# Two outlook-attention layers in fp32: bands of an image in one read, loads of x on another queue, and the first pair's transposed copies kept in idle buffers

## The chip, the core and the metric

The kernel runs on one core of one Trainium2 chip. The metric is device time in microseconds (us) from start to end of one execution, and the median of several executions is compared. All numbers are fp32.

The engines of a core are named as the profile names them: PE (TensorE, the matrix array), DVE (VectorE), ACT (ScalarE), POOL (GpSimd) and SP (SyncE, which only issues transfers here). ACT issues transfers too. An engine executes its own instructions in order; the engines wait for each other and for transfers through semaphores. SBUF is the on-chip memory of 128 partitions, PSUM the memory that PE writes.

## The reference

The input x has 8 images of 56 x 56 positions and 384 channels. Two layers follow each other, each of the form x + conv(groupnorm(x)) with 32 groups.

```
# layer 0, 12 heads of 32 channels, kernel 3 x 3, padding 1
v    = x @ Wv.T                               # padded by 1 in both directions
a    = (x @ Wa.T) as (position, head, 9, 9)
attn = softmax(a * 32 ** -0.5, last axis)
out  = for each position, head:  attn (9 x 9) @ the 3 x 3 patch of v
y    = fold(out)                              # adds each of the 9 rows at its offset
x    = x + y @ Wo.T
# layer 1, 6 heads of 64 channels, 9 weights a head
a    = softmax((x @ W_attn + b_attn) as (position, head, 9))
y    = sum over the 9 of the patch of v, weighted by a
x    = x + y @ W_proj + b_proj
```

The group norm needs the mean and the variance of 12 channels over a whole image before the first position of that image can be projected.

## The kernel before, in words

**Tiling.** Two images make a pair; a column of a pair has R = 112 rows, which lie on the partitions. There are four pairs of W = 56 columns. A block is XB = 4 columns, so a pair has NBLK = 14 blocks. The 384 channels are NCH = 3 chunks of 128.

**Statistics of pair 0.** Before the loop, `stats_load` (L389) reads a block of x as xr, in rows, on SP's queue. `stats_chunk` (L395) transposes it chunk by chunk on PE, with four transposes for each chunk. ACT copies the result to xt (L409), DVE takes the statistics (L411), and SP stores xt to xT in DRAM (L413). The pools hold two buffers for xr and two for xt. `norm_params` (L233) then averages over the groups with products by `gmat`, all nine pairs of chunks, and makes scale and bias. The group size is 12 and a group that crosses from one chunk to another reaches only the next chunk, so the blocks of gmat with chunk numbers two apart hold zeros. For the other pairs the same chunks are worked through inside the loop, one for each step, while the pair before is computed (`upkeep`, L651).

**Layer 0's loop.** A step is one column. `attend` (L476) makes three groups of 9 x 36 logits from xn and wa_t into PSUM banks; DVE, ACT and POOL make the softmax; the product with wv_t gives v, which ACT sends to the table vtab. `presum` and `fold` (L513, L543) sum rows and send the folded weights wt to a table ztab in DRAM. `load` (L457) brings back block g of xT as xin on SP's queue, and `normed` (L465) scales it into xn, which holds eight columns; `load(g)` stands six steps and `normed(g)` two steps ahead of the block's first column. Every seven columns `fetch_v` (L566) reads patches of v as vp, and `fetch` (L574) reads the bands of weights z, puts the contraction (pc) and the output product (po) in a list of jobs due four steps later, and reads the residual xres from xT. z has one buffer for each image of the pair, vp two.

**Bands.** `bands` (L304) reads one image's z in three transfers, given by `GROUPS0` (L88) as ranges of partitions and of target rows: partitions 0 to 48 with rows 0 to 5, 48 to 80 with rows 0 to 7, and 80 to 128 with rows 3 to 7. What is not read stays at the zeros that POOL writes into both z at the start (L455).

**Order.** PE's instructions are kept in program order, and so are the clears of the tables (`fill`, L176). All else is ordered by a scheduler, so a transfer can stand far from its place in the text. In the built program every transfer signals one of eight completion semaphores, which SP's and ACT's transfers take in turn; an issue also waits until the transfer that used its semaphore before has landed.

**Layer 1** works in the same way with its own tables and is not touched.

Of the kernel before, what the change touches and what calls it, by code (L numbers as in the profile page):

```python
# [8 lines left out]
F32 = mybir.dt.float32  # L9
# [6 lines left out]
def two_outlook_layers(  # L16
# [68 lines left out]
    PY1, NPY1, SX1, SY1 = 8, 7, PX + 2, 10  # L85
    ROW1 = HEADS1 * PX

    GROUPS0 = (((0, 48), (0, 5)), ((48, 80), (0, 7)), ((80, P), (3, 7)))  # L88
    GROUPS1 = (((0, 45), (0, 5)), ((45, 90), (3, 8)))


# [28 lines left out]

    def transpose(*args, **kwargs):
        tc.keep_in_program_order(nc.tensor.transpose(*args, **kwargs))  # L122


    ident = const.tile([P, P], F32, name="ident")
# [50 lines left out]
    def fill(table, first, dims, width):  # L176

        src = zeros[: dims[0][1], :width]
        if len(dims) > 1:
            src = src.unsqueeze(1).to_broadcast([dims[0][1], dims[1][1], width])  # L180
        tc.keep_in_program_order(
            nc.sync.dma_start(bass.AP(table.tensor, table.offset + first, [*dims, [1, width]]), src)
        )

    def clear_v(table, sx, pad):

        line = sx * C
        part = line // 12
        fill(table, 0, [[(R + GAP) * line, NPX + 1], [part, 12 * GAP]], part)
        fill(table, GAP * line, [[line, R], [C, pad]], C)  # L190
        fill(
            table, ((NPX - 1) * (R + GAP) + GAP) * line + (sx - pad) * C,
            [[line, R], [C, pad]], C,
        )

    def clear_weights(table, line, part, sx, slot, row, first, e, ep):
        fill(table, 0, [[part, MARGIN * line // part]], part)
        fill(table, (MARGIN + R) * line, [[part, (MARGIN + 1) * line // part]], part)
        top = MARGIN * line
        fill(table, top, [[line, R]], first * row)  # L200
        fill(table, top + (first + e) * row, [[line, R], [slot, sx]], (ep - e) * row)

    def clears():

        yield 0, lambda: clear_v(vtab0, SX0, 2)

        yield 0, lambda: fill(
            ztab0[0], MARGIN * LINE0 + FIRST0 * ROW0, [[LINE0, R], [SLOT0, 2]], E0 * ROW0
        )
        for n, t in enumerate(ztab0):  # L210
            yield (1, 2 * PX, 3 * PX)[n], lambda t=t: clear_weights(
                t, LINE0, 366, SX0, SLOT0, ROW0, FIRST0, E0, EP0
            )
# [11 lines left out]
    eps_t = const.tile([P, 1], F32, name="eps_t")  # L225
    nc.gpsimd.memset(eps_t, EPS)

    def weight(pool, src, n, name):
        t = pool.tile([P, NCH, n], F32, name=name)
        nc.sync.dma_start(t, src.rearrange("(i p) n -> p i n", p=P))  # L230
        return t

    def norm_params(st, name, params, key):  # L233

        mv = stat.tile([P, NCH, IMG, 2], F32, tag="mv", name=f"mv_{name}")

        def over_groups(src, what):
            pg = ps.tile([P, NCH, IMG], F32, tag="t", name=f"p{what}_{name}")
            for j in range(NCH):
                for i in range(NCH):  # L240
                    matmul(
                        pg[:, j, :], gmat[:, i, j * P : (j + 1) * P], src[:, i, :],
                        start=(i == 0), stop=(i == NCH - 1),
                    )
            g = stat.tile([P, NCH, IMG], F32, tag=what, name=f"{what}_{name}")
            nc.vector.tensor_copy(g, pg)
            return g

        for i in range(NCH):
            for b in range(IMG):  # L250
                nc.vector.bn_aggr(mv[:, i, b, :], st[:, i, b, :, :])
# [6 lines left out]
        nc.vector.tensor_add(part, part, mv[:, :, :, 1])  # L258
# [59 lines left out]
    class Jobs:  # L318


        def __init__(self):
            self.queue = []
# [30 lines left out]
    def patch_tiles(name, b):  # L353
        return patch.tile([P, NPY0, C], F32, tag="vp", name=f"vp_{name}_{b}")
# [25 lines left out]
    def layer0(late, pools):  # L380
# [5 lines left out]

        stats, st1s, params, xins, attns, pres, xrs, xts = {}, {}, {}, {}, {}, {}, {}, {}

        def stats_load(pair, blk):  # L389
            nm = f"{pair}_{blk}"  # L390
            xr = io.tile([P, XB, C], F32, tag="xr", name=f"xr_{nm}")[:R]
            nc.sync.dma_start(xr, xf[pair * R : (pair + 1) * R, blk * XB : (blk + 1) * XB, :])
            xrs[pair, blk] = xr

        def stats_chunk(pair, blk, i, alone):  # L395

            nm = f"{pair}_{blk}"
            if blk == 0 and i == 0:
                stats[pair] = stat.tile([P, NCH, IMG, NBLK, 6], F32, tag="st0", name=f"st0_{pair}")
            if i == 0:  # L400
                xts[pair, blk] = io.tile([P, NCH, XB, R], F32, tag="xt", name=f"xt_{nm}")
            xr, xt = xrs[pair, blk], xts[pair, blk]
            if alone:
                pt = bank(P, 0, XB * R).rearrange("p (m r) -> p m r", m=XB)
            else:
                pt = ps.tile([P, XB, R], F32, tag="t", name=f"pt_{nm}_{i}")
# [5 lines left out]
            if i == NCH - 1:  # L412
                nc.sync.dma_start(  # L413
                    xTs[pair][:, :, blk * XB * R : (blk + 1) * XB * R], xt.rearrange("p i m r -> p i (m r)")
                )
                del xrs[pair, blk], xts[pair, blk]

        stats_load(0, 0)
        for blk in range(NBLK):
            if blk + 1 < NBLK:  # L420
                stats_load(0, blk + 1)
            for i in range(NCH):
                stats_chunk(0, blk, i, True)
        for _ in norm_params(stats.pop(0), "0_0", params, 0):
            pass

# [22 lines left out]
                )  # L449
        for t in banks:  # L450
            nc.vector.memset(t[:, BANK - NP0 + NL :], 0.0)
        wv_t = weight(fixed, wv0, C, "wv0_t")
        wo_t = weight(late_w, wo0, C, "wo0_t")
        for z in zs:
            nc.gpsimd.memset(z, 0.0)  # L455

        def load(g):  # L457
            pair, blk = divmod(g, NBLK)
            xins[g] = io.tile([P, NCH, XB, R], F32, tag="xin", name=f"xin_{g}")
            nc.sync.dma_start(  # L460
                xins[g].rearrange("p i m r -> p i (m r)"),
                xTs[pair][:, :, blk * XB * R : (blk + 1) * XB * R],
            )
# [187 lines left out]
        def upkeep(step):  # L651

            pair, c = divmod(step, W)
            while clearing and clearing[0][0] <= step:
                clearing.pop(0)[1]()
            if pair + 1 < NPAIR:
                blk, i = divmod(c - 3, NCH)
                if 0 <= c and i == 0 and blk < NBLK - 1:
                    stats_load(pair + 1, blk + 1)
                if 3 <= c and blk < NBLK:  # L660
                    stats_chunk(pair + 1, blk, i, False)
                elif NBLK * NCH + 3 <= c < NBLK * NCH + 6:
                    if c == NBLK * NCH + 3:
                        making["0"] = norm_params(stats.pop(pair + 1), f"0_{pair + 1}", params, pair + 1)
                    next(making["0"])
            g, j = divmod(step + XB + 2, XB)
            if j == 0 and g < NPAIR * NBLK:
                load(g)
            g, j = divmod(step + 2, XB)
            if j == 0 and g < NPAIR * NBLK:  # L670
                normed(g)

        load(0)
        load(1)
        normed(0)
        LAG = 3
        for step in range(NPAIR * W + LAG):
# [329 lines left out]
```

## Time and profile before

| | |
|---|---|
| median of 12 runs | 3619.28 us (3612.08 to 3640.48) |
| the profiled execution | 3618.46 us, its span 3616.5 us |
| PE busy | 3465.0 us, 96% |
| DVE, ACT, POOL busy | 53%, 32%, 27% |
| DMA moved | 799.46 MB, 221 GB/s on average |
| SP's queue (q1), ACT's queue (q10) | 602.16 MB, 192.66 MB |
| first product of layer 0's loop | at 88.45 us |

PE's busy time is that of instructions in flight, so a busy PE is not a PE at its peak. An engine's idle time before an instruction is put down to what released it, in the form "<-DMA xr<-in_x": released by the transfer that wrote xr from in_x. The form "LABEL x12" means twelve instructions in one line. L119 and L122 are the helper lines by which all products and all transposes are recorded, so they are told apart by their tiles. "bank<-wa_t,xn" is a product of layer 0's logits, "pt<-ident,xr" a transpose inside the loop and "bank<-ident,xr" one of the start.

### The profile page before, as it was taken

The page shows a single profiled execution, that of the slowest core. Times are in us where ns is not written, and L with a number is a line of the kernel's source. Part 1 is how long each engine was busy: PE and PEld are TensorE (multiplying, and loading weights), DVE is VectorE, ACT ScalarE, POOL GpSimd, SP SyncE. Part 2 cuts the span into 40 slices and gives each one's busy share as a digit, 9 for nine tenths or more (in the row PEclk, how much of TensorE's full clock was granted, in tenths as well). Part 3 has the DMA queues.
Part 4 walks back from the last instruction along what each step waited for, and adds up shares of the span by engine and source line. Part 5 has one row for each costly group of instructions (what it writes and reads, how often), then busy time and mean ns, then how long its engine had stood idle before and what let it go on. Part 6 is the DMA issues. An engine that isn't in the chain of part 4 may idle for free. (4 is left out here: it accounts for less than half of the span.)

```text
span 3616.5 us, 72464 instructions
## 1 busy us (share of the span) xinstructions
PE 3465.0 (96%) x29078; PEld 2379.5 (66%) x29078; DVE 1915.8 (53%) x4648; ACT 1167.8 (32%) x2727; POOL 982.0 (27%) x1409
## 2 busy tenths in 40 slices
PE   5999899999999999999999999979999999999998
PEld 4667667767777677777777776645565565556555
DVE  3766566666776676666766666622222222222222
ACT  3333332333233233323322332223333333334332
POOL 2544333433444433343444444410000000000000
PEclk5999999999999999999999999989999999999998
DMA  8699999989999889999878887887787888788876
GB/s 283 202 261 260 251 255 233 221 207 241 252 228 235 213 217 236 248 256 216 205 192 203 211 216 194 193 241 186 207 222 204 223 216 217 198 223 209 220 190 154
DMA packets 694302, 799.46 MB, mean 221 GB/s; under 512 B 304270, under 2 KB 647374, under 8 KB 689870
## 3 DMA queue, kind: packets, MB, share of 16 engines
q1 hardware_dynamic: 359438, 602.16, 63.6%
q10 hardware_dynamic: 334528, 192.66, 22.0%
q8 instruction: 229, 3.75, 0.5%
q14 instruction: 107, 0.88, 0.1%
HBM read 473.04 MB, written 321.66 MB: 220 GB/s over the span
## 5 line engine op out<-in xcount | busy, mean ns | idle before, releaser
L119 PE MATMUL bank<-wa_t,xn 128*112 128x288 f32 x4032 | 1086.0, 409 | 3.3 <-ACT xn L471 2.2
L119 PEld LDWEIGHTS bank<-wa_t,xn 128*112 128x112 f32 x4032 | 693.9, 177 | 254.3 <-issue 32.8
L510 POOL TENSOR_TENSOR at<-at,den 112x972 f32<-112x972 f32 x224 | 503.7, 2249 | 1229.3 <-DVE den L509 1195.9
L119 PE MATMUL po<-yT,wo_t 128*128 128x448 f32 (+1 forms) x2304 | 821.8, 496 | 5.4 <-DVE x1t L621 4.8
L119 PEld LDWEIGHTS po<-yT,wo_t 128*128 128x128 f32 x2304 | 434.8, 191 | 294.8 <-issue 190.6
L119 PE MATMUL pc<-z,vp 121*32 121x49 f32 (+1 forms) x17664 | 492.5, 255 | 56.1 <-issue 25.6
L119 PEld LDWEIGHTS pc<-z,vp 121*32 121x32 f32 (+1 forms) x17664 | 445.1, 131 | 135.6 <-issue 107.4
L119 PE MATMUL bank<-wc_t,xn 128*128 128x438 f32 x1176 | 489.3, 553 | 3.0 <-ACT xn L740 3.0
L486 DVE TENSOR_REDUCE mx<-bank 112x36 f32<-112x324 f32 x672 | 326.5, 486 | 283.4 <-PE bank L119 277.3
L119 PE MATMUL bank<-wv_t,xn 128*128 128x384 f32 x1176 | 417.6, 492 | 2.6 <-DVE at L487 1.9
L487 DVE TENSOR_TENSOR at<-bank,mx 112x324 f32<-112x324 f32 x672 | 329.2, 490 | 20.7
L491 ACT ACTIVATE at<-at 112x972 f32<-112x972 f32 x224 | 227.0, 1013 | 337.1 <-DVE at L487 321.3
L119 PEld LDWEIGHTS bank<-wc_t,xn 128*128 128x128 f32 x1176 | 218.3, 195 | 177.9 <-issue 165.3
L824 POOL TENSOR_TENSOR at<-at,den 112x378 f32<-112x378 f32 x32 | 30.2, 944 | 1118.1 <-DVE den L823 699.5
L740 ACT ACTIVATE xn<-x1t,bias,scale 128x168 f32<-128x168 f32 (+4 forms) x498 | 213.8, 504 | 322.0 <-DMA x1t<-x 214.8
L119 PEld LDWEIGHTS bank<-wv_t,xn 128*128 128x128 f32 x1176 | 219.0, 190 | 141.9 <-issue 18.7
L899 DVE SCALAR_TENSOR_TENSOR x1t<-po,bo_t,x1t 128x448 f32<-128x448 f32 (+1 forms) x192 | 120.2, 626 | 333.5 <-PE po L119 333.5
L533 POOL TENSOR_TENSOR pre<-at,at 112x108 f32<-112x108 f32 (+1 forms) x440 | 236.3, 537 | 138.7 <-DVE wt L556 124.3
L555 ACT COPY wt<-pw 112x120 f32<-112x120 f32 x224 | 58.0, 259 | 657.8 <-PE pw L119 563.8
L779 DVE TENSOR_TENSOR lgt<-bank,ba_t 128x54 f32<-128x54 f32 x196 | 41.4, 211 | 429.0 <-PE bank L119 429.0
L503 DVE TENSOR_TENSOR d<-at 112x432 f32<-112x432 f32 x224 | 141.1, 630 | 225.4 <-ACT at L491 222.4
L600 ACT COPY yT<-pc 128x294 f32<-128x294 f32 x256 | 103.8, 407 | 375.8 <-PE pc L119 364.3
(81 smaller groups left out, 2841.1 us busy)
## 6 DMA issues: line engine op xcount, KB each, us to landing
vp<-vtab SPq DMA_DIRECT2D x64, 1536.0 KB
ztab<-wt ACTq DMA_DIRECT2D x336, 183.8 KB
vp<-vtab SPq DMA_DIRECT2D x64, 945.0 KB
z<-ztab SPq DMA_DIRECT2D x64, 630.0 KB
xr<-in_x SPq DMA_DIRECT2D x56, 672.0 KB
xT<-xt SPq DMA_DIRECT2D x56, 672.0 KB
xin<-xT SPq DMA_DIRECT2D x56, 672.0 KB
xres<-xT SPq DMA_DIRECT2D x32, 1176.0 KB
```

The costliest lines, as they stand in the source:

```text
L119: tc.keep_in_program_order(nc.tensor.matmul(*args, **kwargs))
L486: nc.vector.tensor_reduce(mx[:, pi, :], pl.rearrange("r q a -> r a q"), AX.X, ALU.max)
L487: nc.vector.tensor_tensor(at[:, pi], pl, mx[:, pi, :].unsqueeze(1).to_broadcast([R, K2, PH]), ALU.subtract)
L491: nc.scalar.activation(at, at, AF.Exp, scale=SCALE0)
L503: nc.vector.tensor_add(d4, at[:, :, 0:4], at[:, :, 4:8])
L510: nc.gpsimd.tensor_tensor(at, at, den.unsqueeze(2).to_broadcast([R, K, K2, PH]), ALU.mult)
L533: nc.gpsimd.tensor_tensor(dst, terms[0], terms[1], ALU.add)
L555: nc.scalar.copy(mid[:, 0 : E0 : E0 - 1, :], pw[:, 0 : E0 : E0 - 1, :])
L600: nc.scalar.copy(yT[:, :, :, b, rows_of], pc.rearrange("p i n y m -> p i m (n y)"))
L740: nc.scalar.activation(to[:, i, :, rows], x1ts[g][:, i, lo - first : hi - first, rows], AF.Identity, bias=bias[:, i, b : b + 1], scale=sca ...
L779: nc.vector.tensor_add(staged[-1][1][:, len(staged[-1][0])], pa[:, :NA1], ba_t)
L899: nc.vector.scalar_tensor_tensor(res, po[:, :n], bo_t[:, j : j + 1], res, ALU.add, ALU.add)
```

## The change

- `GROUPS0` becomes one group: 128 partitions with all seven target rows. z is read in one transfer for each image.
- Loads of xin, and loads of xr for pairs 1 to 3, are issued by ACT.
- In the start, pair 0's transposed blocks go to fourteen buffers that are idle then (`homes`): the two of xin, the two of xt, parts of the patch buffer, both z, yT, xres and the two of x1t. xr has four buffers in the start, two of them in the second patch buffer. The stores to xT are issued in the loop's text, two in each step (`keep_block` in `upkeep`), blocks 0 and 1 last. Blocks 0 and 1 are normalised from their homes, without a load.
- The clears of vtab and of the first ztab are written at steps 3 to 5, wo's load at step 3, and POOL's clear of z at step 8.
- `over_groups` leaves out the two products with blocks of gmat two chunks apart.
- SP's loads in the start and the stores `keep_block` are kept in program order.

```diff
-    GROUPS0 = (((0, 48), (0, 5)), ((48, 80), (0, 7)), ((80, P), (3, 7)))
+    GROUPS0 = (((0, P), (0, 7)),)
 ...
-        yield 0, lambda: clear_v(vtab0, SX0, 2)
-        yield 0, lambda: fill(
+        yield 3, lambda: clear_v(vtab0, SX0, 2)
+        yield 4, lambda: fill(
 ...
-            yield (1, 2 * PX, 3 * PX)[n], lambda t=t: clear_weights(
+            yield (5, 2 * PX, 3 * PX)[n], lambda t=t: clear_weights(
 ...
-                for i in range(NCH):
+                near = [i for i in range(NCH) if abs(i - j) < 2]
+                for i in near:
 ...
+        def keep_block(pair, blk):
+            tc.keep_in_program_order(
                 nc.sync.dma_start(
-                    xTs[pair][:, :, blk * XB * R : (blk + 1) * XB * R], xt.rearrange("p i m r -> p i (m r)")
+                    xTs[pair][:, :, blk * XB * R : (blk + 1) * XB * R],
+                    xts.pop((pair, blk)).rearrange("p i m r -> p i (m r)"),
                 )
+            )
 ...
+        homes = [
+            block_tile("xin", 0, 0),
+            block_tile("xin", 0, 1),
+            block_tile("xt", 0, 2),
+            block_tile("xt", 0, 3),
+            *blocks_in(first_vp[0], 2),
+            *blocks_in(z_flat[1], 3),
+            *blocks_in(z_flat[0], 1, NCH * NA0),
+            *blocks_in(projected("first").rearrange("p i m b y -> p (i m b y)"), 1),
+            *blocks_in(late_w.tile([P, NCH, T], F32, tag="xres", name="xres_first").rearrange("p i t -> p (i t)"), 1),
+            *first_x1t,
+        ]
+        xts.update({(0, blk): home for blk, home in enumerate(homes)})
+        more = first_vp[1][:, : 2 * XB * C].rearrange("p (k m c) -> p k m c", k=2, m=XB)
+        def first_load(blk):
+            xr = more[:R, blk // 2 % 2] if blk % 2 else xr_tile(0, blk)
+            stats_load(0, blk, sync, xr)
+        sync = InOrder(nc.sync)
+        NXR = 4
+        for blk in range(NXR - 1):
+            first_load(blk)
         for blk in range(NBLK):
-            if blk + 1 < NBLK:
-                stats_load(0, blk + 1)
+            if blk + NXR - 1 < NBLK:
+                first_load(blk + NXR - 1)
             for i in range(NCH):
-                stats_chunk(0, blk, i, True)
+                stats_chunk(0, blk, i)
+            if blk == 1:
+                wv_t = weight(fixed, wv0, C, "wv0_t", sync)
 ...
-            nc.sync.dma_start(
+            nc.scalar.dma_start(
                 xins[g].rearrange("p i m r -> p i (m r)"),
 ...
             pair, c = divmod(step, W)
+            if pair == 0:
+                for n in (2 * step, 2 * step + 1):
+                    if n < NBLK:
+                        keep_block(0, (n + 2) % NBLK)
+                if c == 3:
+                    sync.dma_start(wo_t, wo0.rearrange("(i p) n -> p i n", p=P))
+                if c == 8:
+                    for z in zs:
+                        nc.gpsimd.memset(z, 0.0)
 ...
-                    stats_load(pair + 1, blk + 1)
+                    stats_load(pair + 1, blk + 1, nc.scalar, xr_tile(pair + 1, blk + 1))
 ...
-            if j == 0 and g < NPAIR * NBLK:
+            if j == 0 and 1 < g < NPAIR * NBLK:
                 load(g)
 ...
-        load(0)
-        load(1)
+        xins.update({blk: homes[blk] for blk in range(2)})
         normed(0)
```

The helper `InOrder` passes each call on to its engine and keeps the instruction in program order; `blocks_in` cuts block-sized pieces out of a buffer; `block_tile` and `xr_tile` take a buffer from the pool.

More of the change, by code (lines that the diff above doesn't have):

```diff
@@ L122, in transpose, with __init__, __getattr__ @@
         tc.keep_in_program_order(nc.tensor.transpose(*args, **kwargs))
+    class InOrder:
+        def __init__(self, engine):
+            self.engine = engine
+        def __getattr__(self, name):
+            op = getattr(self.engine, name)
+            return lambda *args, **kwargs: tc.keep_in_program_order(op(*args, **kwargs))
     ident = const.tile([P, P], F32, name="ident")
@@ L226, in two_outlook_layers, with weight @@
     nc.gpsimd.memset(eps_t, EPS)
-    def weight(pool, src, n, name):
+    def weight(pool, src, n, name, queue=nc.sync):
         t = pool.tile([P, NCH, n], F32, name=name)
-        nc.sync.dma_start(t, src.rearrange("(i p) n -> p i n", p=P))
+        queue.dma_start(t, src.rearrange("(i p) n -> p i n", p=P))
         return t
@@ L239, in over_groups @@
             for j in range(NCH):
-                for i in range(NCH):
+                near = [i for i in range(NCH) if abs(i - j) < 2]
+                for i in near:
                     matmul(
                         pg[:, j, :], gmat[:, i, j * P : (j + 1) * P], src[:, i, :],
-                        start=(i == 0), stop=(i == NCH - 1),
+                        start=(i == near[0]), stop=(i == near[-1]),
                     )
@@ L387, in layer0, with block_tile, stats_load, xr_tile @@
         stats, st1s, params, xins, attns, pres, xrs, xts = {}, {}, {}, {}, {}, {}, {}, {}
[L389 to L392, printed above, removed]
+        def block_tile(tag, pair, blk):
+            return io.tile([P, NCH, XB, R], F32, tag=tag, name=f"{tag}_{pair}_{blk}")
+        def stats_load(pair, blk, queue, xr):
+            queue.dma_start(xr, xf[pair * R : (pair + 1) * R, blk * XB : (blk + 1) * XB, :])
             xrs[pair, blk] = xr
-        def stats_chunk(pair, blk, i, alone):
-            nm = f"{pair}_{blk}"
+        def xr_tile(pair, blk):
+            return io.tile([P, XB, C], F32, tag="xr", name=f"xr_{pair}_{blk}")[:R]
+        def stats_chunk(pair, blk, i):
             if blk == 0 and i == 0:
                 stats[pair] = stat.tile([P, NCH, IMG, NBLK, 6], F32, tag="st0", name=f"st0_{pair}")
-            if i == 0:
-                xts[pair, blk] = io.tile([P, NCH, XB, R], F32, tag="xt", name=f"xt_{nm}")
+            if i == 0 and pair:
+                xts[pair, blk] = block_tile("xt", pair, blk)
             xr, xt = xrs[pair, blk], xts[pair, blk]
-            if alone:
+            if pair == 0:
                 pt = bank(P, 0, XB * R).rearrange("p (m r) -> p m r", m=XB)
             else:
-                pt = ps.tile([P, XB, R], F32, tag="t", name=f"pt_{nm}_{i}")
+                pt = ps.tile([P, XB, R], F32, tag="t", name=f"pt_{pair}_{blk}_{i}")
             for j in range(XB):
@@ L412, in stats_chunk @@
             if i == NCH - 1:
+                del xrs[pair, blk]
+                if pair:
+                    keep_block(pair, blk)
+        def keep_block(pair, blk):
+            tc.keep_in_program_order(
                 nc.sync.dma_start(
-                    xTs[pair][:, :, blk * XB * R : (blk + 1) * XB * R], xt.rearrange("p i m r -> p i (m r)")
-                )
-                del xrs[pair, blk], xts[pair, blk]
-        stats_load(0, 0)
+                    xTs[pair][:, :, blk * XB * R : (blk + 1) * XB * R],
+                    xts.pop((pair, blk)).rearrange("p i m r -> p i (m r)"),
+                )
+            )
@@ new lines, in blocks_in @@
+        def blocks_in(flat, n, at=0):
+            size = NCH * XB * R
+            for k in range(n):
+                yield flat[:, at + k * size : at + (k + 1) * size].rearrange(
+                    "p (i m r) -> p i m r", i=NCH, m=XB
+                )
+        first_vp = [patch_tiles("first", n).rearrange("p n c -> p (n c)") for n in range(2)]
+        z_flat = [z.rearrange("p n e -> p (n e)") for z in zs]
+        first_x1t = [
+            late_w.tile([P, NCH, 4, R], F32, tag="x1t", name=f"x1t_first_{n}", bufs=2) for n in range(2)
+        ]
@@ new lines, in layer0 @@
+        homes = [
[9 more added lines that the diff above has]
+            *first_x1t,
+        ]
@@ L419, in layer0 @@
+        assert len(homes) == NBLK
+        xts.update({(0, blk): home for blk, home in enumerate(homes)})
[7 more added lines that the diff above has]
+            first_load(blk)
         for blk in range(NBLK):
[L420 to L421 removed]
+            if blk + NXR - 1 < NBLK:
+                first_load(blk + NXR - 1)
@@ L451, in layer0 @@
             nc.vector.memset(t[:, BANK - NP0 + NL :], 0.0)
[L452 to L455, printed above, removed]
+        wo_t = late_w.tile([P, NCH, C], F32, name="wo0_t")
         def load(g):
@@ L653, in upkeep @@
             pair, c = divmod(step, W)
+            if pair == 0:
+                for n in (2 * step, 2 * step + 1):
[6 more added lines that the diff above has]
+                        nc.gpsimd.memset(z, 0.0)
             while clearing and clearing[0][0] <= step:
@@ L658, in upkeep @@
                 if 0 <= c and i == 0 and blk < NBLK - 1:
-                    stats_load(pair + 1, blk + 1)
+                    stats_load(pair + 1, blk + 1, nc.scalar, xr_tile(pair + 1, blk + 1))
                 if 3 <= c and blk < NBLK:
-                    stats_chunk(pair + 1, blk, i, False)
+                    stats_chunk(pair + 1, blk, i)
                 elif NBLK * NCH + 3 <= c < NBLK * NCH + 6:
```

## The prediction

> **What bounds the kernel now.** I read the slices of the page first, then stretches, then the timeline of the slow stretch, then PE's waits.
>
> ```profile
> PE   5999899999999999999999999979999999999998
> PEclk5999999999999999999999999989999999999998
> DMA  8699999989999889999878887887787888788876
> GB/s 283 202 261 260 251 255 233 221 207 241 252 228 235 213 217 236 248 256 216 205 192 203 211 216 194 193 241 186 207 222 204 223 216 217 198 223 209 220 190 154
> ```
>
> PE (TensorE) is full everywhere except in slice 1 (the first 90 us) and at the border of the layers. In slice 1 DMA moves the most bytes and the granted clock is half. The stretches say the same:
>
> ```profile
> 40.00:60.00 20.00, 8.91 (x45) 7.91 (x45) 7.76 (x24) 5.78 (x12) 0.00 (x0) 0.50 0.91 298
> 60.00:80.00 20.00, 11.46 (x55) 9.98 (x53) 10.35 (x32) 7.19 (x13) 0.00 (x0) 0.50 0.93 306
> ```
>
> Columns: stretch, PE, PE loads, DVE, ACT, POOL busy, clock, DMA share, GB/s. No engine is busy beyond half; DMA is at 0.9. For layer 0's main loop:
>
> ```profile
> 88.00:2350.00 2262.00, 2227.60 (x19512) 1594.06 (x19512) 1529.91 (x3780) 697.49 (x1364) 921.64 (x1337) 1.00 0.90 226
> ```
>
> PE idles 34.4 of 2262 us there: nothing but these 34 us, or PE work itself, can be won in the loop. The timeline of the statistics of pair 0:
>
> ```profile
> 58.59 2.48 PE L122 MATMUL bank<-ident,xr 112*128 112x112 f32 x12 [5.15 <-DMA xr<-in_x]
> ...
> 68.61 0.51 SPq L413 DMA_DIRECT2D xT<-xt  x1
> 69.17 2.19 SPq L460 DMA_DIRECT2D xin<-xT  x2
> ...
> 72.28 2.48 PE L122 MATMUL bank<-ident,xr 112*128 112x112 f32 x12 [4.26 <-DMA xr<-in_x]
> ```
>
> The 12 transposes of a block take 2.48 us, but blocks come every 4.8 us (the first at 9.98, the last at 72.28, 13 apart): each block's load shares the DMA with the store of its transposed copy. PE's waits:
>
> ```profile
> PE bank L122 <- DMA xr<-in_x: 30.3, 10, 5.1
> PE pc L119 <- DMA z<-ztab: 22.5, 13, 3.3
> PE pt L122 <- DMA xr<-in_x: 16.7, 3, 12.0
> ```
>
> The first is the start; the third is the same load later, inside the loop, 12.0 us of it at 443 us. SP's queue shows why:
>
> ```profile
> 400.55 23.94 SPq L308 DMA_DIRECT2D z<-ztab  x6
> 425.04 0.57 SPq L609 DMA_DIRECT2D xres<-xT  x1
> ...
> 443.20 0.52 SPq L392 DMA_DIRECT2D xr<-in_x  x1
> ```
>
> Six band reads held SP for 24 us, and the load of x stood behind them.
>
> [...] ACT stood 6.44 us at 125.89 behind its own ztab<-wt issue. [...] between 1000 and 1400 us packets of 1536 bytes, vp's on 128 partitions among them, took 77 ns on average, those of 1680 bytes into 48 partitions 165 ns (68 at the shortest). [...]
>
> **The parts.** All is summed against the profiled execution (3618.46 us, span 3616.5; the median 3619.28 is 0.8 higher).
>
> (a) Stores of pair 0 leave the statistics: 14 of 0.69 MB. Also gone: the two loads xin, and wo and the clears move behind. What is left until the last block: wa 1.49, wv 0.59, xr 13 x 0.69 = 8.9, together 11.0 MB. In the built order the second load, into a buffer that shares memory with the setup, waits for the third setup matmul, so all but the first load start at about 9.4 us (where wa was issued before). At 306 GB/s (the stretch above) 11.0 MB take 36 us[...]. By PE: the second block lands near 16 (it shares with wa), then 12 blocks of 2.48 start the last at 46. I take 48 for the start of the last block's transposes against 72.28: **-24.3** (-20 to -27; four buffers may leave gaps, and packets without stores beside them may be quicker).
>
> (b) over_groups skips the two blocks of gmat that are zero: 7 of 9 products, 14 records for 18. At the start, after the last mv, 14 records ran in 3.15 us; 6 remain: -1.8. The gvar group of 18 took 3.97: -0.9. **-2.7**.
>
> (c) The other seven norm_params are on the full PE:
>
> ```profile
> L119 PE MATMUL pgmean<-mv,gmat 128*128 128x2 f32 x144 | 18.8, 260 | 2.3 <-DVE mv L251 2.3
> L119 PE MATMUL pgvar<-part,gmat 128*128 128x2 f32 x144 | 18.4, 260 | 1.0 <-DVE part L258 1.0
> ```
>
> Less the first call's 4.3 and 4.0, (18.8 - 4.3) / 126 = 0.115 us a record; 7 x 2 x 4 x 0.115 = 6.4. Some stands in waits for DVE: **-5** (-2 to -6.4).
>
> (d) xin 2 and 3 go into buffers that hold blocks 0 and 1 until those are stored, and the built order puts those stores last on SP, behind the 2.4 MB clear of ztab (issued after step 5) and pair 1's first store. ACT issues both loads only after step 7's v, and step 8 needs six activations of block 2. Worked out: the clear lands about 12 us after step 5 ends, near the end of step 6 or early in 7 (steps are 6.5 to 7 us here); block 0's store 4 us later; the load takes 4 us, the activations 6 x 0.47 = 2.8 (twelve took 5.69 at 87.27). PE waits about 8 us at step 8; what stands behind the loads on ACT (wt copies, exp of step 8) waits along, under the same gap. Gone in exchange is the 6.44 us stand of ACT above, which cost PE about 3 us (1.08 and 1.43 at 128 and 131). **+5** (0 to +12).
>
> (e) POOL clears z now after the stores of blocks 6 to 9 and before its first multiply: 2 x 4.02 us that had lain idle in the start. Stores are issued from about 47 us; eight of them and two xr loads, 6.9 MB, end near 70, so POOL is free at about 77. The first multiply came 14 us after PE began the loop, and PE would begin at 88.45 - 27 = 61.5: due at 75.5. pw of step 0 waits for it with some 1.6 us of slack. **+1** (0 to +6).
>
> (f) 39 loads xr and 54 loads xin leave SP; per band pair SP issues 2 reads, not 6. The 12.0 + 4.7 us of pt's wait should mostly go, and some of the 3.6 us of vp and z waits before 300 us: **-13** (-4 to -20). What is late next is ACT's own work.
>
> (g) Those 93 issues now stand on ACT: 0.35 to 0.57 us each, some 45 us on an engine busy 697 of 2262, hidden under PE unless it waits. Eight completion semaphores go round among all DMAs, so an issue waits for an earlier transfer, at times one of SP's. Behind it stand v, yT, wt and xt copies that free PSUM. **+4** (0 to +16; the rival below).
>
> (h) Bands: 128 x 7 in place of 48 x 5 + 32 x 7 + 48 x 4, per row of patches 896 units for 656: 2352 KB for 1722, 64 times, +41 MB. Packets stay 1024 per read. Before: 384 x 165 + 256 x 189 + 384 x 109 ns (means of the packet records, same stretch) over 16 engines is 9.6 us. After, between 1536 bytes at 77 and 3136 at 175 ns (xres, 128 partitions): 127 ns, 8.1 us. At the 189 ns that 2352 bytes take on 32 partitions: 12.1 us. Twice per 70 us, DMA share 0.90 becomes 0.86 or 0.97. I take the first, at **0**: a read begins about 35 us ahead of its use, under PE. The 9.6 MB of stores moved into the first steps count as hidden too, apart from (d) and (e); without that cover they cost 9.6 / 300 GB/s = 32 us, the whole gain of (a).
>
> Sum: -24.3 - 2.7 - 5 + 5 + 1 - 13 + 4 = -35.0: 3618.5 - 35.0 = **3583.5 us**.
>
> **Rivals.** (1) The start is won, the loop is not: xr's stalls come back as stands of ACT or at SP, (f) is 0, (g) +8. -24.3 - 2.7 - 5 + 5 + 1 + 8 = -18: 3600. For: 12.0 of the 16.7 us are one event. Against: its cause in SP's queue is plain. (2) The bytes count, not the packets: 41 MB in 2262 us are 18 GB/s on 226, at a share of 0.90 about the ceiling of 251. Bands land late; if 60 reads miss by 0.4 us, 25 us go: 3608. Against: the 48-partition packets were the slow ones. (3) **Slower:** ACT stands for its loads. ACT's waits on vtab<-v were 46.6 us in 10 for wt alone, 4.7 each; if each of 93 loads stands so long and PE has 3.7 us of slack in its banks, PE loses 1 us a load: +93 for (g)'s 4, 3673. It decides from 39 / 93 = 0.42 us a load. Against: ACT is 31% busy, and its stand of 6.4 us at 125 cost PE only 3. (4) The change doesn't do what it says: SP stores run beside the last loads anyway, the start gains 10: 3598.
>
> **How the numbers follow.** Forecast 0.60, (1) 0.16, (2) 0.08, (3) 0.08, (4) 0.08. The forecast's own terms span 3560 to 3606, seldom all on one side; 3564 to 3608 takes in (1), (4) and the near part of (2). A run can tell 0.3%, 11 us, from no change. Slower by more: (3), 0.07. Within: its near side and half of (2), 0.05. Faster: the rest, 0.88.
>
> **What would show it.** Right: the last transposes by the start's bank near 48 us and the first product with wa near 61; no xT<-xt beside them but at the end; pgmean 112 records; a PE gap of some 8 us by xn at step 8 near 120 us; no pt wait on xr of over 3 us; packets of 2352 bytes near 127 ns. Wrong: a start past 55 us, PE waiting on ACT in the loop, z waits in layer 0 of over 10 us in all.

## The result, and the profile after

| | before | after |
|---|---|---|
| median | 3620.86 us (32 runs, 3612.08 to 3640.48) | 3565.5 us (8 runs, 3558.46 to 3578.88) |
| ratio, 95% interval | | 0.9848 [0.9831, 0.9864] |
| profiled execution (span) | 3618.46 (3616.5) | 3569.28 (3567.5) |
| PE busy, mean clock | 3465.0, 0.977 | 3442.5, 0.985 |
| DMA | 799.46 MB, 221 GB/s | 839.34 MB, 235 GB/s |
| first product of layer 0's loop | 88.45 us | 63.68 us |

The change makes the kernel 1.5% faster: 55 us by the medians and 49 by the profiled executions, where 35 were forecast. The time is in the range of 3564 to 3608, 1.5 us from its lower end. First the slices of the page after:

```profile
PE   7799999999999999999999999989999999999998
PEclk8899999999999999999999999999999999999999
DMA  7999888688887778887667776787878878878886
GB/s 240 274 296 279 268 275 275 212 256 251 286 252 222 259 240 251 260 260 266 209 194 229 238 218 207 247 265 177 218 204 214 222 204 218 206 201 220 217 219 160
```

Three things differ from the slices of before. Slice 1 of PE is 7, not 5. Slice 2 is now 7 as well, so something was put in there. And the DMA row reads mostly 6 to 8 in layer 0 where it read mostly 8 to 9, though the row below shows more bytes. The start in the timeline after (start, duration, engine and line, operation, in brackets the idle time before it and its releaser; SPq and ACTq are the issuing of transfers; vp_first is a patch buffer that serves the start):

```profile
47.28 2.48 PE L122 MATMUL bank<-ident,xr 112*128 112x112 f32 x12 [0.21 <-DMA xr<-in_x]
49.55 1.84 PE L122 MATMUL bank<-ident,vp_first 112*128 112x112 f32 x12
...
63.68 2.71 PE L119 MATMUL bank<-wa_t,xn 128*112 128x288 f32 x5 [2.24 <-ACT xn L529]
64.58 4.02 POOL L721 MEMSET z<- 128x4704 f32 x1 [33.91 <-ACT xn L529]
```

The last block's transposes begin at 49.55 for 72.28, and the first product 24.8 us earlier than before. The stretch that moved 298 GB/s before, and the one ahead of it:

```profile
20.00:40.00 20.00, 14.02 (x94) 12.30 (x92) 13.63 (x42) 11.05 (x23) 6.80 (x9) 0.91 1.02 308
40.00:60.00 20.00, 12.98 (x72) 11.88 (x71) 12.91 (x43) 8.17 (x15) 0.00 (x0) 0.68 1.03 348
```

From 40 to 60 us PE is busy 12.98 of 20 us for 8.91. The last load of a block is issued at 40.20 us and the first store of one at 40.57, so the loads ran at the 308 GB/s of the first line, and the 348 of the second are in large part stores. PE's waits after, over the whole run (what for, us in total, times, longest):

```profile
PE pc L119 <- DMA z<-ztab: 22.7, 13, 3.8
PE bank L119 <- ACT xn L529: 17.0, 2, 14.8
...
PE bank L122 <- DMA vp_first<-in_x: 8.0, 5, 2.1
...
PE bank L122 <- DMA xr<-in_x: 5.4, 5, 2.2
```

The waits for z stay at 22.7 for 22.5, and none of them lies in layer 0's loop: they are layer 1's. The transposes of the start wait 13.4 us, on vp_first and xr, for 30.3. The wait "pt <- DMA xr" (16.7) is gone. A single wait of 14.8 us has come. It is the one in slice 2:

```profile
101.84 6.90 SPq L192 DMA_DIRECT2D ztab<-zeros  x4
...
111.14 13.30 SPq L435 DMA_DIRECT2D xT<-xin  x2
...
129.27 3.32 ACTq L518 DMA_DIRECT2D xin<-xT  x2
133.91 3.58 ACT L529 ACTIVATE xn<-xin,bias,scale 128x224 f32<-128x224 f32 x7 [13.00 <-DMA xin<-xT]
135.00 5.29 PE L119 MATMUL bank<-wa_t,xn 128*112 128x288 f32 x12 [14.77 <-ACT xn L529]
```

SP has issued the 2.4 MB clear of a ztab by 108.7. Behind it, in one line of 13.30 us, come the issues of the stores of blocks 0 and 1 ("xT<-xin"). By the semaphore records of the trace the clear, issued at 108.42, had landed at 123.91. The store of block 0, whose issue began at 111.14, landed at 129.20; that of block 1 was not issued before 123.93, because the clear held its completion semaphore. (In this trace SP and ACT use eight such semaphores, 241 or 242 times each. Between two issues on one of them all 16 updates of the first transfer's landing are on record in 1907 of 1926 cases, 8 to 15 of them in the other 19.) At 129.27 the load into block 0's buffer goes out, it lands at 133.88, the activations follow, and PE goes on at 135.00. Last the border of the layers, in SP's queue, before and then after:

```profile
2369.96 21.14 SPq L308 DMA_DIRECT2D z<-ztab  x6
```

```profile
2337.29 5.40 SPq L320 DMA_DIRECT2D z<-ztab  x2
```

The six band reads held SP for 21 us, and the last read of xres, two stores of x and two loads of x1t came only after them; two band reads hold it for 5.4.

To see where the time went I compared, column by column, when POOL begins the softmax multiply (L568 after), against the same column in the profiled execution of before. Negative is ahead of before, in us. e1 to e12 are the experiments below. "Layer 1, 8" is tile 8 of layer 1 (when DVE adds the bias to its logits), just past the border; past it, in layer 1, the traces wander by some 10 us and more, though no edit touches it.

Two things limit what the table can show. Each trace is one execution: those of e1 and e9 are the fastest of their four, that of e3 the slowest of its eight. And before and after were not traced beside the rest, which ran on chips where before was slower (the medians stand under "The experiments"). How far that reaches is shown by e8, which is before with seven group products for nine: though its edit only takes work away, it falls back by 7 us from column 11 to 34 and by 9 past column 38. A difference of that size between two traces is not yet an effect of an edit.

| column | before, at | after | e1 | e2 | e3 | e4 | e5 | e6 | e8 | e9 | e10 | e11 | e12 |
|---|---|---|---|---|---|---|---|---|---|---|---|---|---|
| 0 | 102.5 | -24.6 | -23.8 | 0.7 | 8.1 | -19.1 | -22.3 | -24.3 | -2.5 | -27.4 | -24.1 | -22.6 | -20.4 |
| 7 | 153.0 | -29.4 | -20.1 | 0.3 | 5.1 | -16.9 | -27.0 | -21.7 | 0.1 | -30.0 | -27.1 | -27.3 | -25.2 |
| 11 | 183.4 | -5.1 | -11.1 | 0.3 | 5.6 | -3.2 | -6.3 | -8.4 | -0.4 | -14.5 | -21.3 | -6.1 | -1.7 |
| 34 | 413.1 | -6.4 | -12.8 | -0.2 | 10.2 | -5.9 | 6.3 | -3.8 | 6.6 | -17.5 | -3.9 | 32.9 | 9.3 |
| 38 | 470.0 | -21.5 | -27.7 | -15.5 | -2.1 | -5.2 | -6.8 | -20.3 | 6.3 | -30.7 | -18.7 | 31.5 | -4.2 |
| 223 | 2346.8 | -30.5 | -38.4 | -22.4 | 0.0 | 10.6 | 3.9 | -22.0 | 15.3 | -41.8 | -29.5 | 187.2 | -6.9 |
| layer 1, 8 | 2439.7 | -43.1 | -50.3 | -34.5 | 2.1 | 12.3 | 5.3 | -33.9 | 15.1 | -53.4 | -40.4 | 204.3 | -14.9 |

So of what the start gains, the stand at column 8 takes 24 us back by column 11. Then 15 us come at columns 34 to 38, 9 in the rest of the loop and 12.6 around the border.

### The profile page after: what moved, and what is told of

It is laid out like the page before. It is cut to its first block, busy times and chain, and to the rows that moved or that the text cites. A ratio compares the mean times of both kernels' runs of the same rounds, so it can differ in the third digit from the quotient of the medians.

```text
span 3567.5 us, 72091 instructions
## 1 busy us (share of the span) xinstructions
PE 3442.5 (96%) x29014; PEld 2361.7 (66%) x29014; DVE 1918.7 (54%) x4648; ACT 1162.7 (33%) x2727; POOL 985.4 (28%) x1409
## 2 busy tenths in 40 slices
DMA packets 691452, 839.34 MB, mean 235 GB/s; under 512 B 302190, under 2 KB 595374, under 8 KB 687022
## 3 DMA queue, kind: packets, MB, share of 16 engines
q10 hardware_dynamic: 361504, 258.73, 27.1%
## 5 line engine op out<-in xcount | busy, mean ns | idle before, releaser
L568 POOL TENSOR_TENSOR at<-at,den 112x972 f32<-112x972 f32 x224 | 504.6, 2253 | 1158.3 <-DVE den L567 1101.7
L119 PE MATMUL pc<-z,vp 121*32 121x49 f32 (+1 forms) x17664 | 488.9, 255 | 47.8 <-DMA z<-ztab 22.7
```

The source lines that it names most:

```text
L119: tc.keep_in_program_order(nc.tensor.matmul(*args, **kwargs))
L568: nc.gpsimd.tensor_tensor(at, at, den.unsqueeze(2).to_broadcast([R, K, K2, PH]), ALU.mult)
```

## The experiments

The chips differ: before had medians of 3635.6 us beside e1 to e4, 3652.9 beside e5, e6, e9 and e10, and 3649.9 beside e8, e11 and e12. So each ratio is to before on the same chip.

**One part alone.** The bands alone (e2), the loads on ACT alone (e3), and the start alone (e4).

e2, before with

```diff
-    GROUPS0 = (((0, 48), (0, 5)), ((48, 80), (0, 7)), ((80, P), (3, 7)))
+    GROUPS0 = (((0, P), (0, 7)),)
```

> The kernel before with the bands alone changed: one read of 128 partitions with all seven target rows for each image. Theory A (in the loop and at the border of the layers the reads of z held SP's queue; fewer and quicker reads free it): PE's wait on xr (16.7 us) falls below 4 us and the border gains 5 to 10 us: 3621 - 22 = 3599 (3592 to 3605). Theory B (the loads had to leave SP's queue to be on time): the 12 us wait on xr stays or moves to another block: 3614 to 3621. Theory C (the 41 MB more are felt): slower than 3625. Packets of 2352 bytes take about 104 ns, as in the changed kernel, in A and B.

Measured: 3589.2 us, ratio 0.9874 [0.9846, 0.9902]. The bands alone carry most of the gain. In the table they cure the stall at columns 34 to 38 (-15.3), gain 7 us in the rest of the loop (6 of them from column 50 to 76, where two of before's waits for xr lie), and 12 around the border.

e3, before with

```diff
-            nc.sync.dma_start(xr, ...)
+            (nc.scalar if pair else nc.sync).dma_start(xr, ...)
 ...
-            nc.sync.dma_start(            # load: xin
+            nc.scalar.dma_start(
```

> The kernel before with the loads alone changed: xin, and xr of pairs 1 to 3, are issued by ACT; bands stay three reads. Theory A (six band reads in front of xr on SP were the cause, and either cure is enough): PE's wait on xr falls below 4 us, the border of the layers stays as before: 3621 - 15 = 3606 (3600 to 3611). Theory B (bands alone gave the loop's gain): no more than 5 us from this edit: 3614 to 3621. Theory C (ACT stands for its loads, the slower rival of the prediction): 3625 or more, with PE waiting on ACT's copies.

Measured: 3618.57 us, 0.9956 [0.9928, 0.9983]. The loads on ACT alone cure the same stall (-12.3 from column 34 to 38), and 4 us more from column 50 to 76, lost again by column 223; the border stays as before. (Column 0 is 8 us late there, with one wait of 10.5 us for a load in the start, which the edit does not touch.) In the profile PE has no wait on ACT worth naming in 100 to 500 us:

```profile
PE pc L119 <- issue: 5.9, 6, 2.4
PE pw L119 <- POOL pre L531: 2.9, 4, 1.3
PE bank L119 <- DVE at L487: 2.0, 2, 1.4
PE pc L119 <- DMA z<-ztab: 1.0, 1, 1.0
```

e4, after with the other parts undone:

```diff
-    GROUPS0 = (((0, P), (0, 7)),)
+    GROUPS0 = (((0, 48), (0, 5)), ((48, 80), (0, 7)), ((80, P), (3, 7)))
 ...
-                near = [i for i in range(NCH) if abs(i - j) < 2]
+                near = list(range(NCH))
 ...
-            nc.scalar.dma_start(            # xin; xr likewise
+            nc.sync.dma_start(
```

> The changed kernel with the bands back to three reads, the loads of xin and xr back on SP, and all nine products in over_groups: only the start's homes, the later stores and clears are left of the change. Theory A: the first product with wa comes near 66.5 us (63.7 plus 2.7 for the products put back), 22 us ahead of before; the gap at step 8 is of the same kind as in the changed kernel and takes back 10 to 25; the wait on xr stays: 3621 - 22 + 15 = 3614 (3602 to 3622). Theory B (the gap came from loads on ACT, which stands while it waits): no gap of over 5 us at step 8: 3594 to 3602.

Measured: 3627.38 us, 0.9972 [0.9957, 0.9987]. The start alone gains about 20 us and gives nearly all back at column 8, then meets the stall of before. PE's waits in 100 to 500 us show both:

```profile
PE bank L119 <- ACT v L556: 15.1, 1, 15.1
PE pt L122 <- DMA xr<-in_x: 11.3, 1, 11.3
```

The three ratios gain 1.26, 0.44 and 0.28%, together 1.98, and the change gains 1.52. e2 and e3 cure one stall of 12 to 15 us, 0.3 to 0.4%: counted once, the sum agrees, as far as intervals of 0.15 to 0.28 points on each part can say.

**One part undone.** e5 is after with the three band reads of before (the first diff in reverse).

> The changed kernel with the bands back to three reads for each image; start, stores and loads on ACT as changed. Theory A (the wait on xr is cured by the bands or by the loads, either is enough; the border of the layers is won by the bands alone): the steps between 34 and 76 keep their 20 us, the border's 11 us go, DMA share in the loop is back near 0.9: ratio to before 0.9848 + 0.003 = 0.988 (0.9865 to 0.990). Theory B (bands are what the whole loop gained from): the 20 us go too: ratio 0.993 or more.

Measured: 3627.23 us, 0.9934 [0.9904, 0.9964]. Without the single reads more than half of the gain is gone. From column 34 to 38 the loads on ACT still gain 13 us. Past column 38 the trace loses 11 to that of before; e8, on another chip than before too, loses 9 there, so more telling, though still one trace each, is that e6 below, on e5's chip, does 12 us better over these columns with single reads. The border gains nothing (SP's queue stands 22.25 us over six band reads there), where e6 gains 12.

e6 is after with the loads of xin and xr back on SP.

```diff
-            nc.scalar.dma_start(
+            nc.sync.dma_start(
 ...
-                    stats_load(pair + 1, blk + 1, nc.scalar, xr_tile(pair + 1, blk + 1))
+                    stats_load(pair + 1, blk + 1, nc.sync, xr_tile(pair + 1, blk + 1))
```

> The changed kernel with the loads of xin and xr back on SP; bands, start and stores as changed. Theory A (beside single band reads the loads' own queue gives nothing): ratio to before 0.9848 within 0.002; PE's wait on xr in the loop under 4 us; a gap of 10 to 25 us at steps 7 and 8 as before, now with v's copy or xn behind SP's order. Theory B (the queue is worth its own gain): 0.989 or more, with a wait on xr or xn in the loop.

Measured: 3589.44 us, 0.9831 [0.9805, 0.9858], not to be told from the change itself. With single band reads the intervals show no difference by the engine that issues the loads. Nor does the stand at column 8 depend on it; it only takes another name, v's buffer waiting for its store:

```profile
PE bank L119 <- ACT v L556: 17.7, 2, 15.6
```

e8 is before with the group products of neighbouring chunks alone.

```diff
-                for i in range(NCH):
+                near = [i for i in range(NCH) if abs(i - j) < 2]
+                for i in near:
```

> The kernel before with the group products of neighbouring chunks alone (seven in place of nine). Theory A (steps b and c of the prediction, sized by the 8.2 us that the 112 pgmean and 112 pgvar products took less): 7.7 us less, ratio 0.998. Theory B (in the loop PE has other work beside them, only the start counts): 2.7 us less, ratio 0.9993.

Measured: 3645.46 us, 0.9991 [0.9977, 1.0004]. The interval holds both theories and no effect. At the start the trace shows the first product 2.6 us and column 0 2.5 us earlier, as the prediction had it; what it brings in the loop stays open.

**What in the bands is cheap.** e11 keeps the bytes and the packets of 2352 bytes, and goes back to three ranges of partitions. e12 keeps 128 partitions, and makes two reads.

```diff
-    GROUPS0 = (((0, P), (0, 7)),)
+    GROUPS0 = (((0, 48), (0, 7)), ((48, 80), (0, 7)), ((80, P), (0, 7)))   # e11
+    GROUPS0 = (((0, P), (0, 5)), ((0, P), (5, 7)))                         # e12
```

> The kernel after, but the bands of an image in three transfers by ranges of partitions (48, 32, 48), each with all seven rows of targets: the bytes and the packets of 2352 bytes stay as in the kernel after, the ranges and the number of issues are those of before. Theory A (what costs is a short range of partitions): packets of 2352 bytes take 165 to 200 ns, as the 189 of the 32-partition read before, so the bands' packets take about 10.6 us of 16 engines an image in place of 8.4 before and 5.8 after; the DMA share of 1000 to 1400 us rises from 0.77 to 0.95 or more, and the ratio to the kernel before is 0.993 or more, as with three reads in the run before. Theory B (what costs is the short or uneven rows): packets stay near 104 ns, the share near 0.77, ratio 0.985.

> The kernel after, but the bands of an image in two transfers, both of 128 partitions, one with five rows of targets (packets of 1680 bytes) and one with two (672 bytes): the same bytes, twice the issues. Theory A (range of partitions): packets of 1680 bytes near 75 ns in place of 165 in the kernel before, the DMA share of 1000 to 1400 us below 0.82, ratio 0.985 (0.980 to 0.990). Theory B (one transfer in place of several, whatever its shape): the share back near 0.9, ratio 0.993 or more.

Measured: e11 3833.4 us, 1.0503 [1.0488, 1.0519]; e12 3603.86 us, 0.9864 [0.9841, 0.9887]. The same stretch of layer 0's loop in five kernels: before, after, e5, e11, e12 (columns as in the stretches above; the last three are clock, DMA share and GB/s):

```profile
1000.00:1400.00 400.00, 398.15 (x3726) 287.64 (x3725) 271.69 (x676) 128.44 (x251) 158.63 (x233) 1.00 0.91 226
```

```profile
1000.00:1400.00 400.00, 399.36 (x3455) 286.19 (x3454) 277.67 (x691) 125.15 (x243) 160.10 (x234) 1.00 0.77 246
```

```profile
1000.00:1400.00 400.00, 395.79 (x3703) 285.21 (x3702) 268.57 (x668) 126.80 (x248) 160.49 (x233) 1.00 0.92 222
```

```profile
1000.00:1400.00 400.00, 367.51 (x3266) 261.62 (x3268) 250.49 (x621) 113.63 (x225) 148.51 (x215) 0.98 0.99 227
```

```profile
1000.00:1400.00 400.00, 398.82 (x3712) 286.71 (x3711) 272.66 (x680) 128.05 (x252) 160.47 (x233) 1.00 0.82 245
```

The bytes are those of after in e11, yet DMA's engines are full (0.99) and move no more than before. (The expectation's 10.6, 8.4 and 5.8 us count 896 packets for an image; the records have 1024, which makes 12.1, 9.6 and 6.7.) Then PE idles 32 us in 400; its waits up to 2600 us, most of them at the contraction of the bands, begin with

```profile
PE pc L119 <- issue: 92.3, 35, 10.2
PE pc L119 <- DMA z<-ztab: 69.8, 15, 8.3
```

The packet records of the stretch give the means (to within 3 ns, by where the 400 us are begun):

| packets of the bands | bytes | into partitions | mean ns |
|---|---|---|---|
| before | 1680 | 0 to 48 | 165 |
| before | 2352 | 48 to 80 | 189 |
| after | 2352 | 0 to 128 | 104 |
| e11 | 2352 | three ranges | 215 |
| e12 | 1680 | 0 to 128 | 78 |

At the same size, packets take 1.8 and 2.1 times as long into a short range (189 and 215 ns for 104). A fuller DMA alone does not explain it: vp's packets (1536 bytes, 128 partitions, same queue) took 76 ns in before, 75 in after and 74 in e11, though those of xres, which follow the band reads, took 176, 135 and 171. Why a short range costs more, no trace here shows; what the cost goes with is shown: the range. Bytes are refuted as the cause by e11. The number of issues is refuted for the packets by e12 (78 ns, at twice the issues), and in time two issues cost nothing that the intervals show.

**The stand at column 8.** e1 stores blocks 0 and 1 first.

```diff
-                        keep_block(0, (n + 2) % NBLK)
+                        keep_block(0, n)
```

> The changed kernel with one edit: the stores of pair 0's blocks go out in the order 0, 1, 2 ... 13 instead of 2 ... 13, 0, 1. Theory A (the gap at step 8 is the store of blocks 0 and 1, queued on SP behind the 2.4 MB clear, and nothing else): xin 2 and 3 are loaded long before step 8, PE's 14.8 us wait on xn and the half-clock steps after it go, the softmax multiply of step 11 stands some 29 us ahead of the kernel before and not 5; about 20 us off 3565.5: 3545 (3540 to 3551). Theory B (the first steps are short of DMA: 9.6 MB of stores, 3.3 MB of clears and the loads collide, whatever their order): another wait takes the gap's place, at least half of it stays: 3556 to 3566.

Measured: 3572.58 us, 0.9822 [0.9791, 0.9853]. The wait on xn is gone and at column 8 the trace is 8 us ahead of that of after, but at column 11 only 6. POOL's clears of z lay at columns 3 to 5, and by column 7 some 8 us were lost against after; ACT stood later:

```profile
141.03 0.32 SPq L192 DMA_DIRECT2D ztab<-zeros  x1
...
157.51 1.28 ACTq L619 DMA_DIRECT2D ztab<-wt  x2
158.89 1.01 ACT L549 ACTIVATE at<-at 112x972 f32<-112x972 f32 x1 [10.64 <-issue]
...
160.32 3.22 PE L119 MATMUL bank<-wa_t,xn 128*112 128x288 f32 x6 [4.56 <-ACT v L556]
```

ACT's issue waited for a completion semaphore that the next clear of a ztab, issued at 141.03, still held: it came free after 16 us (the semaphore records have the clear landed at 157.44), and the exp and the copy of v stood behind it.

e9 takes e1 and leaves out the clear of z in the loop, which full-row reads into all partitions make needless, and gives the early loads of x their free buffers in another order.

```diff
-            xr = more[:R, blk // 2 % 2] if blk % 2 else xr_tile(0, blk)
+            xr = more[:R, blk % 2] if blk // 2 % 2 else xr_tile(0, blk)
 ...
-                if c == 8:
-                    for z in zs:
-                        nc.gpsimd.memset(z, 0.0)
```

> The kernel with blocks 0 and 1 stored first, with two edits: POOL's clear of z in the loop is left out (a read of 128 partitions and all seven rows fills z whole), and blocks 0 and 1 are loaded into the two plain xr buffers, blocks 2 and 3 into the patch buffer, so that the second load need not wait for the setup products. Theory A: the 6 us at steps 5 and 6 (pw behind POOL's 2 x 4.02 us) go, and the statistics end some 4 us sooner (the second block lands before 10 us and not at 14.5); ACT's stand behind the second 2.4 MB clear at step 10 stays: 0.9822 - 0.0025 = 0.9797 (0.978 to 0.982). Theory B (the statistics are held by PE's half clock and not by the second load): only the 6 us: 0.9805.

Measured: 3581.54 us, 0.9805 [0.9771, 0.984]. The start is 3 us earlier than in after, the loss before column 7 is gone, and up to the border it is 10 us ahead of after. ACT's stand stays:

```profile
155.10 1.01 ACT L549 ACTIVATE at<-at 112x972 f32<-112x972 f32 x1 [12.51 <-issue]
...
156.54 3.22 PE L119 MATMUL bank<-wa_t,xn 128*112 128x288 f32 x6 [7.05 <-ACT v L556]
```

e10 is e9 with the last fill of each clear cut into three by rows, so that each lands sooner.

```diff
-        fill(table, top + (first + e) * row, [[line, R], [slot, sx]], (ep - e) * row)
+        for r0, r1 in ((0, 32), (32, 64), (64, R)):
+            fill(table, top + r0 * line + (first + e) * row, [[line, r1 - r0], [slot, sx]], (ep - e) * row)
```

> As the kernel without the clear of z and with early loads, and each table's 2.4 MB clear is cut into three transfers of 32, 32 and 48 rows (the same bytes). Theory A (at step 10 ACT stood 7 us because its issue waited for the landing of the whole clear that held its semaphore): that stand falls below 3 us, 5 us less: 0.978 (0.9765 to 0.980). Theory B (the DMA is full there and the clear's bytes themselves are in the way): no change by the cut: within 0.001 of the kernel without it.

Measured: 3578.97 us, 0.9807 [0.9783, 0.9831]: no gain over e9. The stand does go away (-21.3 at column 11 for -14.5), but by column 34 the trace has lost 17 us. PE waited there 9.5 us for ACT's copies of the contraction and 5.3 for DVE; what held these stays open.

e9 beats before by 1.95% [1.6, 2.3], the best ratio of the study, with e10's next to it. Its interval overlaps that of the change, and the 10 us in the table are those of its fastest execution (3564.61 us; the other three took 3579.63 to 3588.48). So that it beats the change is not shown, nor is it for e1.

## Why the prediction was right

By steps, in the trace up to the border (-43.1 us), against the sum of -35:

| step | forecast | measured | from |
|---|---|---|---|
| (a) + (b), start | -27.0 | -24.8 | first product 63.68 for 88.45 |
| (d) gross wait at step 8 | 8 | 14.8 | the wait on xn |
| (d) net | +5 | +20 | from column 7 to 10, 25.1 are lost; before's own stand, gone, is 4.8 |
| (e) clear of z | +1 | 0 | POOL free at 72.5, its first multiply at 77.9 |
| (c), (f), (g), (h), loop and border | -14 | -38.8 | the rest of the table |

- **(a), (b):** right. The last block stands at 49.55 for 48, so (a) gave 22.7; from there to the first product it took 14.1 us for 16.2, so (b) gave 2.0. The rate was 308 GB/s where 306 were taken, and the four buffers left gaps between blocks, which were named as a risk. Two readings in the prediction are off and carry nothing: from 60 to 80 us PE is busy 57%, which is beyond half; and in slice 1 the granted clock was not half throughout, but 0.93 in the first 20 us and 0.50 from 20 to 90. Rival (4), a start of -10, is refuted by e4 too.
- **(d):** the right place and mechanism, too small a size. The first term was the clear: 15.5 us from its issue to its landing for 12. The store of block 0 then took 5.3 for 4, and the load 4.6 for 4. Why the clear took longer is not shown. Then PE lost more than this wait: with 2.8 for v's copy and some 1.5 for POOL, its idle time from column 7 to 11 is 19 us, and 24 to 25 were lost. The mean clock was 0.57 from 135 to 140 us, and the twelve products at 135.00 took 5.29 us, where the twelve at 142.58 took 3.08 at a clock of 1.00: 2.2 us of the difference. What the rest is, is not shown.
- **(f), (g):** the stall went as forecast, -15 at columns 34 to 38 and PE's later 4.7 us of waits for xr too, for -13 in all. (f) named two reasons together, the loads that leave SP and the two reads in place of six, and did not see that either is enough: e3 has the first alone and e2 and e6 the second alone, and all three lose the stall. The loads on ACT cost nothing that the runs can see (e3, and e6 beside the change), so (g)'s +4 is about 0. Nor does DMA carry more for them: from 1000 to 1400 us e3 has a share of 0.90 and 228 GB/s for 0.91 and 226 before.
- **(h):** here the step failed most. It took 127 ns for a packet by interpolating in size; it was 104. It took a share of 0.86; it is 0.77. Of before's packets it took 109 ns for those of 1344 bytes into partitions 80 to 128, but in that mean stand some 2500 packets of other transfers, of a size that took 61 ns in after; without them it is about 138 ns (an estimate from these figures). So the bands went from about 10.3 to 6.7 us an image, where the prediction had 9.6 and 8.1. And it valued the relief at 0. About 12 us came at the border, which no step had: after, e2, e6, e9 and e10, with one read for an image, all gain 11 to 13 from column 223 on; e3, e4, e5 and e8, with three, gain none. Past column 38 after gains 9 in the loop, of which 4.7 are waits for xr and so (f)'s. What single reads give there beside that is not settled: e2 does 9 us better than e3, and e6 12 better than e5, in single traces. The direction, cheaper despite 41 MB more, was right.
- **(c):** the 112 records take 14.5 us for each of pgmean and pgvar where 144 took 18.8 and 18.4, so 8.2 us less as a row. What of that shows in the time is not settled (e8).
- **The rivals:** (1) would have the loop give nothing: it gave 38.8. (2), the bytes decide, is refuted by e2 and e11. (3), ACT stands for its loads, is refuted in the loop by e3. ACT did stand at the start in e1 and e9, not for its loads but for a semaphore that a clear held.

So the profiled execution gained 14 us more than the sum, 49 for 35. Loop and border gave 25 more; step 8 took 15 more and the start 2, while (e) took 1 less: 8 us in all up to the border. The other 6 lie past it, where before's own trace lost some 8 us near its end that no other trace here shows, while 2 us of the lead went in layer 1. That the time came within the range is in part luck: the gain of loop and border, undervalued by 25 us, and the loss at step 8, undervalued by 15, partly offset each other.

## What to carry to other kernels

Read the price of a transfer from packets with the same range of partitions, not from packets of the same size: a read of more bytes into all partitions can be the cheaper one (here packets of 2352 bytes into 128 partitions took 104 ns, those of 1680 into 48 took 165), and it frees the queue of its issuer as well (at the border six reads held SP for 21 us, two for 5.4). When stores leave a bounded stretch, find the first step that needs one of their buffers back and put that store first, ahead of any large transfer in the same queue (in e1 this took PE's wait for xn away; that the whole kernel gains by it is not shown, since another stand came in its place). When two edits might cure one stall, run each alone: here either did.

## What the runs showed of the hardware that was not expected

- Packets of 2352 bytes took 104 ns into 128 partitions and 215 ns in three ranges of 32 to 48 partitions; with them a loop that ran at a DMA share of 0.77 filled DMA to 0.99, and the kernel (e11) became 5% slower than before, and 6% slower than e12, which moves the same bytes on the same chip.
- A clear of 2.4 MB landed 14 to 16 us after its issue, and through the semaphore that it held it stopped an issue of 0.3 us on another engine (ACT) for 9 us in e1 and 11 in e9, and one of SP for 9 in after.
